# A perceiver layer on one core: a state scan written over its input, half of its products on GpSimd, and a small matmul moved to the end of its step

## The chip, the cores and the metric

The kernel runs on one core of a Trainium2 chip. The core has five engines with an instruction stream each: PE (TensorE, matrix products; PEld is its loading of weights), DVE (VectorE), ACT (ScalarE), POOL (GpSimd) and SP (SyncE, which here only issues DMAs). Each engine runs its own instructions in order; semaphores make one wait for another. The metric is the device time in microseconds (us) of one execution.

## The reference: what is computed

Three blocks follow each other on x, 16 sequences of 128 rows by 512 columns, all in float32:

- cross attention: queries from x (normalised), keys and values from a context of 2048 rows for each sequence, 16 heads of 32 columns;
- a Mamba block and an MLP: a projection in to 1024 channels, a causal convolution, the selective state scan, a projection out, a normalisation, a GELU MLP of 2048, and a normalisation;
- a feed-forward block with a shared product and a gated expert product.

The change is in the state scan. In the reference it is

```python
deltaA = jnp.exp(dt[..., None] * A)
deltaBx = dt[..., None] * Bm[:, :, None, :] * x[..., None]
def step(h, xs):
    dA, dBx, C = xs
    h = dA * h + dBx
    y = jnp.einsum('bdn,bn->bd', h, C)
    return (h, y)
```

with 16 states (n) for each of the 1024 channels (d). The scan runs over the 128 rows of a sequence. Every scan step below is one DVE instruction over many rows, not one row.

## The kernel before, in words

**The loop.** All work is laid out by hand in one loop over u (lines 1329 to 1460). Attention takes the first 256 steps (NU = 256): step u handles four heads of 512 context rows. The Mamba block runs behind it. Its 8 groups (g) of two sequences each have 32 scan steps (r), and group g's step r stands in step u = 32 (g + 1) + 22 + r. So scan steps begin at u = 54, run beside attention, and go on through u = 309. From u = 257 on there is no attention; the MLP and feed-forward products ("feeds", line 1355) are given out over the steps instead, and this part, to the end, is called the tail.

**The engines' order.** Each engine runs what the loop issues for it in the loop's order. What happens at which step beside the fixed parts is written in tables (`late`, `behind`, `after`, `inner` and others, lines 1203 to 1269), filled by `put(where, u, function)`.

**One attention step on PE** (in this order): the four scores (L307) into banks[0] to banks[3], at the same time in four row groups of the array; the weighted values of the step before (L385, `avp`); two key or value products into `pa` and `pc` (L244, `x_products`); the transposes of three heads' probabilities back into banks[0] to banks[2] (L357); late products, such as in-projections (L577) or out-projections (L515, L762); and the last one or two key or value products (`y_products`). The fourth head's probabilities go another way: DVE transposes blocks (L337, `tr`), SP stores them to HBM (L341, `trd`) and SP gathers them one step later (L347, `pd`).

**One attention step on DVE**: four maxima over the score banks (L315), the first half scan, sums that read `pc` (L264 for keys, L274 for values), the block transpose, the second half scan, the sums after `y_products`, and what the tables add. On ACT: exponentials (L325), decays (L719), copies of the transposed probabilities (L359), and copies of `pa`.

**One scan step** (lines 692 to 755) covers four states of 128 channels for two sequences, in two halves i = 0, 1 of two states (128 x 512 elements). GpSimd makes w = dt x B (L698) one step ahead, ACT writes the decays into PSUM (L719), DVE scans (L733), DVE multiplies by C (L736), and GpSimd sums over the states (L745, L749). B and C come as broadcasts from HBM (`bc`, L647). The decays lie in the bank `hst`; in the tail the second half has `pc`. Decays are written from column 1 on; column 0 of each sequence must be zero, and `anew` (L712) sets it by a memset of four columns. Since the scan is written over the decays, this is done after every half scan:

```python
flat = h.rearrange("p n t -> p (n t)")
nc.vector.tensor_tensor_scan(
    flat, flat, w.rearrange("p n t -> p (n t)"), 0.0, ALU.mult, ALU.add
)
nc.vector.tensor_tensor(
    w, h, bcs[g * 32 + r, DS][:, i * NH // 2 : (i + 1) * NH // 2, :], ALU.mult
)
anew(h)
```

There are 512 half scans. `anew` is also called once for `hst` before the loop (L1325) and once for `pc` at u = 256 (L1268).

**The time step's product** (`dt_first`, L662 to L675; put into `behind` at L1244) is made once in four scan steps, at u = 3 mod 4: one matmul of 128 x 256 (L665, two PE rows in the profile) into a PSUM bank, then two ACT instructions (L669, L670), one on DVE (L672, the reader of the bank beside L669) and one on GpSimd (L674). `dt_second` (L679, L681) and `dt_third` (L686 to L689) follow in the next two steps. In the loop, `behind` stands after the late products and ahead of `after`, `inner` and the step's `y_products`. During attention its bank is `banks[3]` where no late product has taken it, else `pc`.

The functions that the diff touches and what calls them:

Of the kernel before, what the change touches and what calls it, by code (L numbers as in the profile page):

```python
# [10 lines left out]
ALU = mybir.AluOpType  # L11
# [9 lines left out]
DI, DS, DTR = 1024, 16, 32  # L21
# [9 lines left out]
NH = 4  # L31
# [5 lines left out]
def perceiver_layer(ctx: ExitStack, tc: tile.TileContext, a: dict, out: bass.AP):  # L37
    nc = tc.nc
# [74 lines left out]
    with ExitStack() as es:  # L113
# [15 lines left out]
        banks = [psum.tile([P, 512], FP, tag=f"s{j}", name=f"bank{j}") for j in range(4)]  # L129
# [3 lines left out]
        pc = psum.tile([P, 2, 256], FP, tag="pc", name="pc")  # L133
# [148 lines left out]
        def hold(key, g, pa, tag):  # L282
            n = ND if tag == "tr" else 1
            t = pool.tile([P, 2 * n, 256], FP, tag=tag, name=f"{tag}{key}{g}", bufs=1)[:, 0:2, :]
            nc.scalar.copy(t, pa)
            held[key] = t
# [4 lines left out]
        def y_products(of, g, ph, pa, pc):  # L291
            for i, ps in (((6, pa),), ((3, pc), (4, pa)))[ph]:
                product(of, g, i, ps)

        def y_sums(of, g, ph, pa, pc, tag="u2"):
            if ph == 0:
                hold(of + "u2", g, pa, tag)
            else:
                sums[of](g, 0, 1, pc, held[of + "u2"])
                sums[of](g, 1, 0, None, pa)  # L300
# [237 lines left out]
        zTs, xas, zss, bcs, dts, wts, ysum, wts_in = ({} for _ in range(8))  # L538
# [79 lines left out]
        def silu_second():  # L618
            for v, t in sgs:
                nc.vector.scalar_tensor_tensor(t, v, 0.0, t, ALU.min, ALU.subtract)  # L620
# [85 lines left out]
        def states(g, r, i):  # L706

            return pc if i and 32 * (g + 1) + LAG + r > NU else hst

        def anew(h):  # L710

            nc.vector.memset(h.rearrange("p n (b t) -> p (n b) t", b=GB)[:, :, 0:1], 0.0)  # L712
# [16 lines left out]
        def scan(g, r, i):  # L729
            ec, q = divmod(r, 4)  # L730
            w, h = wts[g, r][i], states(g, r, i)
            flat = h.rearrange("p n t -> p (n t)")
            nc.vector.tensor_tensor_scan(  # L733
                flat, flat, w.rearrange("p n t -> p (n t)"), 0.0, ALU.mult, ALU.add
            )
            nc.vector.tensor_tensor(  # L736
                w, h, bcs[g * 32 + r, DS][:, i * NH // 2 : (i + 1) * NH // 2, :], ALU.mult
            )
            anew(h)

            if q == 0 and i == 0:
                ysum[g, ec] = w
            elif (q, i) == (0, 1):
                s = ssm.tile([P, 2, GT], FP, tag="ysum", name="ysum", bufs=1)
                nc.gpsimd.tensor_tensor(s, ysum[g, ec], w, ALU.add)  # L745
                ysum[g, ec] = s
            else:
                s = ysum[g, ec]
                nc.gpsimd.tensor_tensor(s, s, w, ALU.add)  # L749
            if (q, i) == (3, 1):  # L750
                y = ysum[g, ec][:, 0, :]
                nc.gpsimd.tensor_tensor(y, y, ysum[g, ec][:, 1, :], ALU.add)
                nc.gpsimd.tensor_tensor(y, y, xas[g, ec], ALU.add)
                nc.gpsimd.tensor_tensor(zss[g, ec], y, zss[g, ec], ALU.mult)
                del ysum[g, ec], xas[g, ec], dts[g, ec]
# [44 lines left out]
        def flat(ps):  # L800
            return ps.rearrange("p k q -> p (k q)")
# [3 lines left out]
        def bank():  # L805
            return free_banks.pop(0)

        def give_back(*ps):
            free_banks.extend(ps)
# [393 lines left out]
        late, after, inner, middle, loads, head, behind, between, weights = ({} for _ in range(9))  # L1203
# [27 lines left out]
        for g in range(NG):  # L1231
            p = 32 * (g + 1)
# [87 lines left out]
        ps = banks[2]  # L1320
# [8 lines left out]
        for u in range(last):  # L1329
            live = u < NU  # L1330
            g, r = divmod(u - 32 - LAG, 32)
# [3 lines left out]
            makes = 0 < made < B * SB  # L1335
# [64 lines left out]
            if scans:  # L1400
                scan(g, r, 0)
# [16 lines left out]
            free = banks[NP:]  # L1418
# [14 lines left out]
            if scans:  # L1433
                scan(g, r, 1)
            for f in middle.get(u, ()):
                f()
            for f, ps in zip(after_turns, places):
                if live:
                    f(ps)
                else:  # L1440
                    ps = bank()
                    f(ps)
                    give_back(ps)
            for f in behind.get(u, ()):
                n = len(late.get(u, ()))
                if live and n < len(free):
                    ps = free[n]
                else:
                    ps = flat(pc) if makes else banks[2] if live else bank()
                f(ps)  # L1450
                if not live:
                    give_back(ps)
            for f in after.get(u, ()):
                f()
            for f in inner.get(u, ()):
# [1 line left out]
            if makes:  # L1457
                y_products(of, made, phase, pa, pc)
                y_sums(of, made, phase, pa, pc)
            silu_second()  # L1460

        while fed < len(units):
# [74 lines left out]
```

## Time and profile before

| what | before |
|---|---|
| median of three timed runs | 3677.24 us (3677.19 to 3677.81) |
| the profiled execution's own time | 3673.68 us |
| its span, first to last instruction | 3671.8 us |
| PE, DVE, ACT, POOL busy | 3622.8, 2704.5, 2422.8, 2135.5 us |
| granted PE clock, mean | 0.997 |
| HBM | 185 GB/s over the span |

How to read it: a row of the costliest groups names the line, engine and operation, what is written and read, the count, then the busy time of the group in us and the mean length of one in ns, and at the end the idle time of the engine just ahead of these instructions with what ended most of it. A row of a timeline has the start in us, the length in us, engine, line and operation, and in brackets the idle time ahead and what ended it. Matmuls overlap, so PE's busy time is a union, and a mean length of a matmul is longer than its share of the time.

### The profile page before, as it was taken

Reading aid. Unit: us, or ns where it says so; the run is one execution under the profiler, and the core shown is the slowest. Engines: PE = TensorE matmul, PEld = TensorE weight load, DVE = VectorE, ACT = ScalarE, POOL = GpSimd, SP = SyncE. Lnnn points to the kernel's source line nnn. Section 1 sums busy time; section 2 is a strip of 40 time slices with the busy share of each in tenths; the row PEclk is TensorE's granted clock in tenths of the full one; section 3 lists DMA queues with packets and bytes.
Section 4 is the critical chain, followed back from the end, with each engine's and each line's share of the span. In section 5 each row is a group of like instructions: output and inputs, shape, how many; then the busy total and the mean of one; then the engine's idle time right before and its main releaser. Section 6 shows DMA issues by size and latency. Waiting matters only on the chain. (4 is left out here: it accounts for less than half of the span.)

```text
span 3671.8 us, 70944 instructions
## 1 busy us (share of the span) xinstructions
PE 3622.8 (99%) x25096; PEld 2750.8 (75%) x25096; DVE 2704.5 (74%) x4902; ACT 2422.8 (66%) x5928; POOL 2135.5 (58%) x2097
## 2 busy tenths in 40 slices
PE   9999999999999999999999999999999989999999
PEld 7878787778777877788778877887778766655655
DVE  4444445897879787878788878887887768778843
ACT  4555556787777776777687767776777675545422
POOL 2111214675767676766676667766776657667720
PEclk9999999999999999999999999999999999999999
DMA  3322333665666666665666575657565678576752
GB/s 122 99 90 94 106 108 127 193 200 185 203 199 193 194 188 212 196 197 171 223 196 193 171 243 171 220 162 229 186 213 171 216 233 312 193 278 232 269 176 75
DMA packets 527554, 682.74 MB, mean 186 GB/s; under 512 B 44848, under 2 KB 378960, under 8 KB 526944
## 3 DMA queue, kind: packets, MB, share of 16 engines
q1 hardware_dynamic: 526752, 677.57, 57.0%
q8 instruction: 200, 3.28, 0.3%
q14 instruction: 154, 1.26, 0.1%
q0 software_dynamic: 448, 0.63, 0.1%
HBM read 594.40 MB, written 83.62 MB: 185 GB/s over the span
## 5 line engine op out<-in xcount | busy, mean ns | idle before, releaser
L315 DVE TENSOR_REDUCE nm<-bank 128x1 f32<-128x512 f32 x1024 | 635.4, 682 | 229.2 <-PE bank L307 228.9
L749 POOL TENSOR_TENSOR ysum<-ysum,w 128x512 f32<-128x512 f32 x384 | 501.1, 1305 | 422.9 <-DVE hst L712 258.7
L325 ACT ACTIVATE pr<-bank,nm 128x512 f32<-128x512 f32 x1024 | 689.1, 686 | 66.9 <-DVE nm L315 62.0
L698 POOL TENSOR_TENSOR w<-dx,bc 128x512 f32<-128x512 f32 x512 | 653.2, 1297 | 29.3 <-DMA bc<-bcd 20.9
L733 DVE TENSOR_TENSOR_SCAN hst<-hst,w 128x512 f32<-128x512 f32 x459 | 556.7, 1213 | 38.5 <-ACT hst L719 34.2
L719 ACT ACTIVATE hst<-dt,alog 128x254 f32<-128x254 f32 x918 | 440.1, 479 | 88.9 <-DVE hst L712 70.7
L359 ACT COPY pT<-bank 128x512 f32<-128x512 f32 x768 | 396.5, 587 | 43.6 <-PE bank L357 43.4
L357 PE MATMUL bank<-ident,pr 128*128 128x128 f32 x3072 | 378.2, 273 | 0.8 <-ACT pr L325 0.7
L357 PEld LDWEIGHTS bank<-ident,pr 128*128 128x128 f32 x3072 | 350.5, 141 | 26.3 <-ACT pr L325 3.0
L385 PEld LDWEIGHTS avp<-pT,v 128*32 128x32 f32 x6144 | 207.0, 110 | 196.1 <-issue 193.4
L736 DVE TENSOR_TENSOR w<-hst,bc 128x512 f32<-128x512 f32 x459 | 317.5, 692 | 22.2 <-DMA bc<-bcd 6.5
L307 PE MATMUL bank<-kt,qT 32*128 32x512 f32 x2048 | 305.0, 641 | 5.2 <-ACT pT L359 5.2
L236 POOL TENSOR_TENSOR t<-c,c 128x512 f32<-128x512 f32 x128 | 163.2, 1275 | 239.2 <-PE pc L244 235.1
L385 PE MATMUL avp<-pT,v 128*32 128x128 f32 x6144 | 276.7, 276 | 0.8 <-ACT pT L359 0.7
L244 PE MATMUL pa<-t,ks 128*128 128x256 f32 x1024 | 248.6, 386 | 0.0
L244 PE MATMUL pa<-vs,t 128*128 128x256 f32 x1008 | 244.7, 386 | 0.0
L244 PEld LDWEIGHTS pa<-t,ks 128*128 128x128 f32 x1024 | 185.9, 190 | 36.0 <-issue 11.5
L244 PEld LDWEIGHTS pa<-vs,t 128*128 128x128 f32 x1008 | 185.5, 190 | 34.8 <-issue 10.1
L325 ACT ACTIVATION_READ_ACCUMULATOR pr<-bank,nm 128x1 f32 x1024 | 208.5, 204 | 0.0
L385 PE MATMUL avp<-pd,v 128*32 128x128 f32 x1536 | 204.5, 276 | 0.0
L577 PE MATMUL bank<-zT,win 128*128 128x256 f32 x808 | 185.1, 379 | 0.0
L236 POOL TENSOR_TENSOR t<-c,t 128x512 f32<-128x512 f32 x128 | 163.7, 1279 | 31.7 <-issue 11.9
(321 smaller groups left out, 7392.2 us busy)
## 6 DMA issues: line engine op xcount, KB each, us to landing
bc<-bcd SPq DMA_DIRECT2D x512, 512.0 KB, 4.9
c<-in_ctxT_dram SPq DMA_DIRECT2D x256, 256.0 KB, 5.9
trd<-tr SPq DMA_DIRECT2D x256, 256.0 KB, 4.4
pd<-trd SPq DMA_DIRECT2D x1024, 64.0 KB, 1.9
wf<-in_w_dram SPq DMA_DIRECT2D x124, 512.0 KB, 7.0
wqo<-in_wqkvo_dram SPq DMA_DIRECT2D x128, 256.0 KB, 5.4
win<-in_win_dram SPq DMA_DIRECT2D x128, 256.0 KB, 5.0
wout<-in_wout_dram SPq DMA_DIRECT2D x128, 256.0 KB, 5.9
```

Of the source, the lines that this page charges most:

```text
L236: nc.gpsimd.tensor_tensor(t, x, y, ALU.subtract)
L244: nc.tensor.matmul(ps[:, r, :], l[:, kc, r * P : (r + 1) * P], m[:, kc, :], start=(i in (1, 2, 5) and r == 0 and kc == 0), stop=(r == 1 an ...
L315: nc.vector.tensor_reduce(stats[b][0][j][:, sb, hg : hg + 1], banks[j], AX.X, ALU.max, negate=True)
L325: nc.scalar.activation(pr[:, j, :], banks[j], AF.Exp, bias=nm[j][:, sb, hg : hg + 1], accum_out=sm[:, sb, h : h + 1],)
L357: nc.tensor.transpose(ps[:, i, :], prs[u][:, j, i * P : (i + 1) * P], ident)
L359: nc.scalar.copy(pT, ps)
L385: nc.tensor.matmul(avp[j * HD : (j + 1) * HD, v % 4, :], values(v, i, j), pts[v, j][:, i, :] if j < NP else pds[v][:, :, j - NP, i, :], st ...
L698: nc.gpsimd.tensor_tensor(w, dx.unsqueeze(1).to_broadcast([P, NH // 2, GT]), bcs[g * 32 + r, 0][:, i * NH // 2 : (i + 1) * NH // 2, :], AL ...
L719: nc.scalar.activation(bt(h[:, k, :])[:, :, 1:], bt(dt)[:, :, 1:], AF.Exp, scale=aneg[:, ec, n : n + 1],)
L733: nc.vector.tensor_tensor_scan(flat, flat, w.rearrange("p n t -> p (n t)"), 0.0, ALU.mult, ALU.add)
L736: nc.vector.tensor_tensor(w, h, bcs[g * 32 + r, DS][:, i * NH // 2 : (i + 1) * NH // 2, :], ALU.mult)
L749: nc.gpsimd.tensor_tensor(s, s, w, ALU.add)
```

## The change

Two edits.

- In `scan`, the result goes over w (SBUF) instead of over the decays (PSUM). The product with C then reads w and the broadcast C, both in SBUF, and is made on GpSimd for the first half and on DVE for the second. The memset after each half scan is gone; the zeros of `hst` and `pc` are set once and stay.
- In the loop, the functions in `behind` (the time step's product) are called after `y_products` and `y_sums` instead of ahead of `after`. During attention their bank is `pc` while key and value products are made, and banks[2] in the last attention steps; banks[3] is no longer used for it.

```diff
         def scan(g, r, i):
             ec, q = divmod(r, 4)
             w, h = wts[g, r][i], states(g, r, i)
-            flat = h.rearrange("p n t -> p (n t)")
+            x = w.rearrange("p n t -> p (n t)")
             nc.vector.tensor_tensor_scan(
-                flat, flat, w.rearrange("p n t -> p (n t)"), 0.0, ALU.mult, ALU.add
+                x, h.rearrange("p n t -> p (n t)"), x, 0.0, ALU.mult, ALU.add
             )
-            nc.vector.tensor_tensor(
-                w, h, bcs[g * 32 + r, DS][:, i * NH // 2 : (i + 1) * NH // 2, :], ALU.mult
+            (nc.vector if i else nc.gpsimd).tensor_tensor(
+                w, w, bcs[g * 32 + r, DS][:, i * NH // 2 : (i + 1) * NH // 2, :], ALU.mult
             )
-            anew(h)
...
-            for f in behind.get(u, ()):
-                n = len(late.get(u, ()))
-                if live and n < len(free):
-                    ps = free[n]
-                else:
-                    ps = flat(pc) if makes else banks[2] if live else bank()
-                f(ps)
-                if not live:
-                    give_back(ps)
             for f in after.get(u, ()):
                 f()
             for f in inner.get(u, ()):
                 f()
             if makes:
                 y_products(of, made, phase, pa, pc)
                 y_sums(of, made, phase, pa, pc)
+            for f in behind.get(u, ()):
+                ps = flat(pc) if makes else banks[2] if live else bank()
+                f(ps)
+                if not live:
+                    give_back(ps)
             silu_second()
```

## The prediction, made before the changed kernel was run

> **What bounds the kernel now.** I read the page first: the profiled execution took 3673.68 us around a span of 3671.8 us, 3.56 us below the median of the three timed runs (3677.24 us). All sums below are changes against that one execution; I apply them to the median.
>
> ```profile
> PE 3622.8 (99%) x25096; PEld 2750.8 (75%) x25096; DVE 2704.5 (74%) x4902; ACT 2422.8 (66%) x5928; POOL 2135.5 (58%) x2097
> L749 POOL TENSOR_TENSOR ysum<-ysum,w 128x512 f32<-128x512 f32 x384 | 501.1, 1305 | 422.9 <-DVE hst L712 258.7
> L698 POOL TENSOR_TENSOR w<-dx,bc 128x512 f32<-128x512 f32 x512 | 653.2, 1297 | 29.3 <-DMA bc<-bcd 20.9
> L733 DVE TENSOR_TENSOR_SCAN hst<-hst,w 128x512 f32<-128x512 f32 x459 | 556.7, 1213 | 38.5 <-ACT hst L719 34.2
> L736 DVE TENSOR_TENSOR w<-hst,bc 128x512 f32<-128x512 f32 x459 | 317.5, 692 | 22.2 <-DMA bc<-bcd 6.5
> ```
>
> The reader is to see two things. PE is busy for all but 49 us of the span, so whatever the other engines save, the time can only fall by the places where PE waits. And GpSimd (POOL) waits 258.7 us for the memset L712, the last of the three DVE instructions (scan, product, memset) of each half scan.
>
> So I went through the timeline of PE for the places where a group starts late. From the first scan step to the last attention step (about 615 to 2960 us) there are few kinds. The first, PE and then DVE, around one step's scores:
>
> ```profile
> 2185.26 1.14 PE L307 MATMUL bank<-kt,qT 32*128 32x512 f32 x8
> ...
> 2194.46 1.56 PE L307 MATMUL bank<-kt,qT 32*128 32x512 f32 x8
> ```
> ```profile
> 2194.38 0.48 DVE L672 TENSOR_SCALAR dt<-bank,dtb 128x256 f32<-128x256 f32 x1
> ```
>
> The eight rows of the scores take 1.14 us, but 1.56 us in the step after a time-step product that went to banks[3]: the fourth score must wait until L672 has read that bank, at 2194.86 us. I count 20 such steps, each 1.56 instead of 1.14 us: three of every 32 steps, those where no late product held the free bank.
>
> The second kind, once in 32 steps (six times), is the product into pc two steps after a sequence's end:
>
> ```profile
> 1886.75 1.99 PE L244 MATMUL pc<-c,ks 128*128 128x256 f32 x8 [0.94 <-DVE kt L264]
> ```
> ```profile
> 1883.77 1.22 DVE L733 TENSOR_TENSOR_SCAN hst<-hst,w 128x512 f32<-128x512 f32 x1
> 1885.02 0.69 DVE L736 TENSOR_TENSOR w<-hst,bc 128x512 f32<-128x512 f32 x1
> 1885.79 0.06 DVE L712 MEMSET hst<- 128x4 f32 x1
> 1885.82 0.88 DVE L264 SCALAR_TENSOR_TENSOR kt<-pc,bk,u1k 128x256 f32<-128x256 f32 x2
> ```
>
> PE starts about 1.1 us late, because L264, which empties pc, stands behind scan, product and memset. The third is one wait of 4.71 us at step 253, where DVE's product waits 4.57 us for the broadcast C. By the table of windows, of PE's 49 us of idle time 8.3 lie in the first 50 us, 9 between 640 and 2960, 11.6 between 2960 and 3020 (the 4.71 among them) and 20 in the tail after that. (The late fourth score is no idle time: the other three rows of the array run.)
>
> **The change, part by part.** *Time-step product behind the step's last product.* It is one matmul (two PE rows) before and after; the order of the program shows it moved behind the product into pa, and always into pc while key and value products are made. The fourth score no longer shares a bank with it: 20 x 0.42 = **-8.4 us**. What is late next: pc is written again 3.9 us into the next step, and L672 and ACT's L669 have read it by about 1.3 us, so nothing. ACT's two instructions (0.49 and 0.42 us) move behind the copy of pa, into the next step's start, where ACT idles 0.64 us before avs; the exponentials slip about 0.25 us, and the transposes that need them come 2.5 us later. If that cover failed it would cost 0.25 us x 50 steps = 12 us. GpSimd's u (L674) and DVE's L679 slip with them, unneeded until the step after. It issues no DMA. At step 255 it goes to banks[2] instead of banks[3] and must wait for a copy: at most its own 0.43 us.
>
> *The scan writes over w.* Its row is 1213 ns into PSUM; no row has it into SBUF. From the rows that differ only so, 692 ns for L736 with a PSUM operand and 692 ns for L1022 alone with none, I take 0, with +-20 ns x 512 = 10 us of DVE time as ends, nearly all beside PE. The 512 memsets go: 62 ns and about 80 ns of waiting each. ACT's next decays are then free at the scan's end, 0.83 us sooner.
>
> *First half's product to GpSimd.* DVE loses 256 x 0.692 = 177 us. GpSimd gains 256 products of two SBUF inputs; the nearest rows are L698 and L749, 1.30 us: 333 us. Per 32 steps (1859.01 to 2237.97 us) POOL is busy 260.3 of 379.0 us; 32 x (1.30 + 0.08 wait for its own result) makes it 304. Much of it fits in the wait for DVE that L749 shows: product, then sum, while DVE scans the second half (1.21 us). Behind it on GpSimd stand the context sums for PE. The narrowest is step 165, where t2 ends at 5.65 us and PE wants it at 6.95 us; there the chain starts from DVE's second product, which does not move, so I charge 0. If it did, each 1 us past the margin costs two steps in 32, 12 us in all.
>
> The second half's product stays on DVE, but now reads two SBUF tensors. The trace has such a pair:
>
> ```profile
> 3175.38 0.69 DVE L1022 TENSOR_TENSOR xr<-xr,x 128x512 f32<-128x512 f32 x1
> ```
> ```profile
> 3269.65 1.64 DVE L1022 TENSOR_TENSOR xr<-xr,x 128x512 f32<-128x512 f32 x1
> ```
>
> The first ran while GpSimd was idle, the second while it multiplied (and GpSimd's two L698 took 2.94 instead of 2.50 us). L736 with its PSUM input never left 691 to 694 ns. So each of the 256 remaining products waits 0 to 0.95 us, and GpSimd loses up to 0.69 us per step. On DVE that gives back 0 to 243 us of the 177 + 73 us saved. It comes at the step's end, where DVE idles 0.3 to 1.5 us before the next maxima.
>
> The Trainium skill's GPSIMD Engine Reference, section Engine selection, speaks against the change: elementwise work belongs on VectorE, being about twice as slow on GpSimd. The rows agree on the price, 1305 against 692 ns; by the rule alone 256 x 0.61 = 157 us would be lost. SBUF — State Buffer, section Who interferes with whom, calls the shared read port a lock for a whole instruction; by that the worst wait would be GpSimd's full 1.30 us, 333 us over 256.
>
> *What this leaves of the other waits.* At the six pc waits the chain is 0.83 us shorter: up to -5.0 us. But just ahead stand two small DVE instructions with two SBUF inputs (L483, 0.99 us, and L490, 0.61 us), which already wait for GpSimd, now busier: up to +1.3 us each time, +8. I take **-1 us**. At step 253 the product that waits is now GpSimd's, so ACT and PE go on: up to -4.7 us, and PE's slow stretch after it, at most -3 us. But the next weighted product needs pd:
>
> ```profile
> 2973.81 1.74 SPq L347 DMA_DIRECT2D pd<-trd  x4
> ```
>
> This is issued when the previous transfer lands, whatever DVE does; with the page's 1.9 us to landing it is there at 2977.4 us, and PE came to it at 2978.33 us. So **-1 us**. SP's next broadcast of C must wait for GpSimd's product as well, up to about 6 us into a step; the transfer behind it, trd, is not ready before 7.3 us: 0.
>
> *Tail (57 steps).* The long wait at 3201.3 us is for the copy of xd behind DVE's two halves: 0.8 us sooner, and up to 3 us more if PE's slow stretch after it goes; **-1 us**. Against it stands POOL. From 3260 to 3400 us it is busy 111.7 of 140 us with 16.5 steps; 16.5 x (1.38 + 0.69) makes 146. About 6 us too many, part of which DVE's lighter load and its 20 us of idle time cover: **+2 us**, between 0 and the 20 us of the rival below.
>
> Sum: -8.4 - 1 - 1 - 1 + 2 = -9.4, rounded to **-10 us**: 3663.7 for the profiled execution, **3667 us** for the median.
>
> **Rivals.** (1) *The port takes it back.* The wait of DVE's product lands on the six pc waits and on ACT's path in short steps; 8 us of losses meet 8.4 of gain: about 3676 us, within 3670 to 3684. For it: 102 of 128 L620 began with GpSimd running. Against it: DVE gains 0.83 us ahead of every place where PE waits on it. (2) *Slower: GpSimd becomes the bound in the tail.* If GpSimd cannot hold the pace from 3020 to 3100 and 3260 to 3400 us (79.5 of 80 and 146 of 140 us by the sum above), DVE's scan waits for w, and the FFN work queued behind it on DVE keeps PE's banks; 25 steps x 0.9 us = 22, less 10: 3689 us. It decides once POOL's work per step passes the 8.5 us that a step lasts there. Against it: PE has seven banks of slack, and POOL idles 28 us in that window. (3) *More goes than I count:* all six pc waits, step 253's wait with its slow stretch, and the slow stretch at 3204: -8.4 - 5 - 6 - 4 = -23: 3654 us.
>
> **How the numbers follow.** Forecast (3660 to 3670 us) 0.46; rival 3, 0.14; rival 1, 0.25; rival 2, 0.15. A measurement of this kernel tells 0.2% from no change, 7.4 us. Faster is forecast and rival 3, 0.60; the same is rival 1, 0.25; slower rival 2, 0.15. The range runs from just under rival 3 to rival 1's middle, 3652 to 3679 us, leaving out rival 2 and a fifth of rival 1.
>
> **What would show it.** Right: scores at 1.14 us after every step, L665 into pc alone, second-half L736 between 0.69 and 1.64 us, POOL near 2500 us, PE's idle time in 615 to 2960 us smaller. Wrong: PE waiting for t (L236) or pT in the short steps, DVE's L733 waiting for POOL's w, new PE waits after 3020 us.

## The result, and the profile after

The changed kernel is a little slower, not faster: 3685.70 us median (12 runs, 3679.97 to 3688.74) against 3677.22 us for the kernel before (12 runs, 3674.89 to 3680.99). The ratio is 1.0021, with a 95% interval of 1.0012 to 1.0030: about 8 us, just over the 0.2% that can be told from no change. The profiled execution of the changed kernel took 3679.97 us (span 3678.2 us), the fastest of its 12, 6.29 us above the profiled execution of before.

Behind `scan` the changed kernel's lines are one lower: L748 is the sum that was L749, L954 the feed-forward product that was L955, L819 the load that was L820. The same rows of the page, after (busy time of each engine; then groups with count, busy us, mean ns, idle time ahead and its main releaser):

```profile
PE 3624.0 (99%) x25096; PEld 2746.4 (75%) x25096; DVE 2572.5 (70%) x4134; ACT 2415.9 (66%) x5928; POOL 2501.2 (68%) x2353
...
L748 POOL TENSOR_TENSOR ysum<-ysum,w 128x512 f32<-128x512 f32 x384 | 503.7, 1312 | 149.3 <-DVE w L736 118.4
L733 DVE TENSOR_TENSOR_SCAN w<-hst,w 128x512 f32<-128x512 f32 x459 | 552.1, 1203 | 51.1 <-ACT hst L719 48.4
...
L736 POOL TENSOR_TENSOR w<-w,bc 128x512 f32<-128x512 f32 x256 | 341.1, 1332 | 65.4 <-DVE w L733 65.3
...
L736 DVE TENSOR_TENSOR w<-w,bc 128x512 f32<-128x512 f32 x256 | 236.4, 923 | 9.6 <-DMA bc<-bcd 0.8
```

The engines' totals are as forecast: GpSimd at 2501.2 us, the scan into SBUF no slower (1203 against 1213 ns), GpSimd's wait for the memset gone. The row to stop at is the last one. A product that always took 692 ns with its PSUM input takes 923 ns on average with two SBUF inputs; 125 of the 256 take over 0.75 us, the longest 1.81 us. DVE has 132 us less to do, and PE is as busy as before.

Where the time went is read from the distances of PE's instructions between the two traces. I cut the run into four stretches: up to the scores of step 64; from there to step 250; the end of attention, to the first feed-forward product (L954); and the tail, to the last sixteen expert products. In the profiled executions they changed by -0.3, -1.5, +1.7 and +7.6 us, and what is behind by -1.2.

**Attention stage.** The late fourth score is gone. PE, the scores after such a step:

```profile
2183.40 1.14 PE L307 MATMUL bank<-kt,qT 32*128 32x512 f32 x8
...
2192.08 0.59 PE L665 MATMUL pc<-xd,dtw 128*128 128x256 f32 x2
2192.60 1.14 PE L307 MATMUL bank<-kt,qT 32*128 32x512 f32 x8
```

1.56 us is 1.14 again, and L665 goes into pc. Steps 0 and 28 of each 32 are shorter by 0.42 us. Step 8 gains only 0.23 us on average: ahead of its maxima (at step 136) DVE's product takes 1.31 us in place of 0.69, and L561, the normalisation of x, 1.05 in place of 0.55. And step 18 of each 32 is longer, in all six places. The starts of the scores of such a step and of the next one, before and then after:

```profile
2073.47 1.14 PE L307 MATMUL bank<-kt,qT 32*128 32x512 f32 x8
...
2087.43 1.14 PE L307 MATMUL bank<-kt,qT 32*128 32x512 f32 x8
```
```profile
2070.39 1.14 PE L307 MATMUL bank<-kt,qT 32*128 32x512 f32 x8
...
2085.52 1.14 PE L307 MATMUL bank<-kt,qT 32*128 32x512 f32 x8
```

13.96 us has become 15.13. DVE's timeline at this place, before and after, shows why:

```profile
2073.45 0.69 DVE L736 TENSOR_TENSOR w<-hst,bc 128x512 f32<-128x512 f32 x1
2074.19 0.22 DVE L483 TENSOR_TENSOR sm<-sm,nm 128x64 f32<-128x64 f32 x1
...
2076.44 2.47 DVE L315 TENSOR_REDUCE nm<-bank 128x1 f32<-128x512 f32 x4
```
```profile
2070.36 1.14 DVE L736 TENSOR_TENSOR w<-w,bc 128x512 f32<-128x512 f32 x1
2071.43 1.30 DVE L483 TENSOR_TENSOR sm<-sm,nm 128x64 f32<-128x64 f32 x1
...
2074.86 2.47 DVE L315 TENSOR_REDUCE nm<-bank 128x1 f32<-128x512 f32 x4
```

L483 is tiny and has two SBUF inputs. Before, it started while GpSimd was idle between two sums and took 0.22 us; after, it starts beside the first of GpSimd's two sums and takes 1.30. The maxima (L315) start 4.47 us into the step and not 2.97, the exponentials wait for them, and PE's transposes wait for the exponentials. GpSimd's timeline, before and after:

```profile
2072.58 1.28 POOL L749 TENSOR_TENSOR ysum<-ysum,w 128x512 f32<-128x512 f32 x1
2074.29 1.28 POOL L749 TENSOR_TENSOR ysum<-ysum,w 128x512 f32<-128x512 f32 x1 [0.43 <-DVE hst L712]
```

```profile
2069.68 1.28 POOL L736 TENSOR_TENSOR w<-w,bc 128x512 f32<-128x512 f32 x1
2071.03 2.96 POOL L748 TENSOR_TENSOR ysum<-ysum,w 128x512 f32<-128x512 f32 x2
```

The added product stands where the first sum stood, and both sums now fall into the next step.

**Tail.** From 3400 to 3500 us PE was busy without a break before (100.00 us of 100); after, it has two long waits there, at 3426 and 3497 us, both for feed-forward weights (each from its own view of PE's timeline):

```profile
3426.27 6.59 PE L954 MATMUL pa<-mT,wf 128*128 128x256 f32 x16 [3.25 <-DMA wf<-in_w_dram]
3432.69 3.62 PE L954 MATMUL bank<-mT,wf 128*128 128x256 f32 x16
```
```profile
3497.80 7.15 PE L954 MATMUL bank<-mT,wf 128*128 128x256 f32 x32 [1.77 <-DMA wf<-in_w_dram]
```

The first costs twice: 3.25 us of waiting, and then 16 products that take 6.59 us where the next 16 take 3.62. The profile shows the granted PE clock at 0.50 during these 16 (3426.3 to 3432.1 us), and at 1.00 in the same window before. Measured on the starts of the feed-forward products, the kernel falls back by 6.7 us at the first wait and by 2.0 at the second; all else in the tail comes to -1.1 us. Both loads went out late. SP's issues of a broadcast and of the weights behind it, before and then after; these are the weights of the first wait:

```profile
3409.90 1.04 SPq L647 DMA_DIRECT2D bc<-bcd  x2
3410.99 1.22 SPq L820 DMA_DIRECT2D wf<-in_w_dram  x2
```
```profile
3416.89 2.24 SPq L647 DMA_DIRECT2D bc<-bcd  x2
3419.18 1.22 SPq L819 DMA_DIRECT2D wf<-in_w_dram  x2
```

The weights stand behind a broadcast in SP's order; they are issued 8.2 us later than before, and those of the second wait 12.8 us later (3490.51 and not 3477.68 us). What the broadcast waits for, by the view of SP's waits (us in total, times, longest), before from 3390 to 3425 us and after from 3395 to 3430 us:

```profile
SPq L647 <- POOL w L698: 16.7, 5, 6.1
```

```profile
SPq L647 <- POOL w L698: 21.6, 4, 6.4
```

GpSimd has not yet read the tile that the broadcast is to overwrite. The wait is not new: it grew. In the window of the second line, 3395 to 3430 us, the kernel before has 10.6 us of it, the longest 4.3. From 3400 to 3500 us GpSimd was busy 74.87 us before; it is busy 95.29 us after, all but full.

### The profile page after: what moved, and what is told of

Same layout as the page of the kernel before. It is cut to its first block, busy times and chain, and to the rows that moved or that the text cites. A ratio compares the mean times of both kernels' runs of the same rounds, so it can differ in the third digit from the quotient of the medians.

```text
span 3678.2 us, 70467 instructions
## 1 busy us (share of the span) xinstructions
PE 3624.0 (99%) x25096; PEld 2746.4 (75%) x25096; DVE 2572.5 (70%) x4134; ACT 2415.9 (66%) x5928; POOL 2501.2 (68%) x2353
## 4 chain that ended last, share of the span: by engine, by line
PE 87%; DVE 4%; ACT 3%; POOL 3%; DMA 2%; issue 1%; SPq 0%; DVEq 0%; POOLq 0%
PE pa L244 23%; PE pc L244 17%; PE bank L357 8%; PE bank L307 7%; PE avp L385 7%; PE bank L577 5%; PE bank L985 3%; PE bank L761 2%; PE bank L954 2%; PE bank L1086 2%; PE bank L515 2%; ACT pr L325 1%; POOL w L698 1%; PE pa L954 1%; PE bank L442 1%
## 5 line engine op out<-in xcount | busy, mean ns | idle before, releaser
L315 DVE TENSOR_REDUCE nm<-bank 128x1 f32<-128x512 f32 x1024 | 635.6, 683 | 205.0 <-PE bank L307 204.7
L698 POOL TENSOR_TENSOR w<-dx,bc 128x512 f32<-128x512 f32 x512 | 652.9, 1296 | 32.7 <-DMA bc<-bcd 24.3
L748 POOL TENSOR_TENSOR ysum<-ysum,w 128x512 f32<-128x512 f32 x384 | 503.7, 1312 | 149.3 <-DVE w L736 118.4
L733 DVE TENSOR_TENSOR_SCAN w<-hst,w 128x512 f32<-128x512 f32 x459 | 552.1, 1203 | 51.1 <-ACT hst L719 48.4
L736 POOL TENSOR_TENSOR w<-w,bc 128x512 f32<-128x512 f32 x256 | 341.1, 1332 | 65.4 <-DVE w L733 65.3
L307 PE MATMUL bank<-kt,qT 32*128 32x512 f32 x2048 | 296.0, 640 | 0.5 <-ACT pT L359 0.5
L736 DVE TENSOR_TENSOR w<-w,bc 128x512 f32<-128x512 f32 x256 | 236.4, 923 | 9.6 <-DMA bc<-bcd 0.8
L264 DVE SCALAR_TENSOR_TENSOR kt<-pc,bk,u1k 128x256 f32<-128x256 f32 x256 | 112.2, 480 | 173.5 <-PE pc L244 104.6
L274 DVE TENSOR_TENSOR v<-pc,u1v 128x512 f32<-128x512 f32 x126 | 87.2, 692 | 177.2 <-ACT u1v L285 90.9
```

Of the source, the lines that this page charges most:

```text
L307: nc.tensor.matmul(banks[j], qts[b][rows, hg, :], kts[u // 4, hg][rows, :], start=True, stop=True)
L315: nc.vector.tensor_reduce(stats[b][0][j][:, sb, hg : hg + 1], banks[j], AX.X, ALU.max, negate=True)
L698: nc.gpsimd.tensor_tensor(w, dx.unsqueeze(1).to_broadcast([P, NH // 2, GT]), bcs[g * 32 + r, 0][:, i * NH // 2 : (i + 1) * NH // 2, :], AL ...
L733: nc.vector.tensor_tensor_scan(x, h.rearrange("p n t -> p (n t)"), x, 0.0, ALU.mult, ALU.add)
L736: (nc.vector if i else nc.gpsimd).tensor_tensor(w, w, bcs[g * 32 + r, DS][:, i * NH // 2 : (i + 1) * NH // 2, :], ALU.mult)
```

## The experiments

Each kernel was run beside the kernel before on the same chip. The times together; the last three columns are the change of a stretch against before, in us, from the one profiled execution of each. The attention column (steps 64 to 250) leaves step 22 of each 32 out: PE mostly waits there for a weight transfer (`wqo`), and the six of them together moved by -1.9 to +3.1 us without following the edit.

| kernel | median us | before, median us | ratio, 95% interval | attention | end of attention | tail |
|---|---|---|---|---|---|---|
| changed | 3685.70 | 3677.22 | 1.0021 (1.0012 to 1.0030) | +0.4 | +1.7 | +7.6 |
| 1 move only | 3667.32 | 3674.64 | 0.9983 (0.9974 to 0.9992) | -6.5 | +2.0 | +0.4 |
| 2 scan only | 3691.07 | 3674.64 | 1.0045 (1.0032 to 1.0059) | +7.5 | +2.3 | +8.7 |
| 3 tail products on DVE | 3680.05 | 3674.64 | 1.0014 (1.0005 to 1.0022) | -0.8 | +1.9 | +5.8 |
| 4 broadcasts behind weights | 3680.75 | 3674.64 | 1.0016 (1.0008 to 1.0025) | -0.8 | +2.4 | +6.2 |
| 5 both products on DVE | 3679.74 | 3673.68 | 1.0016 (1.0007 to 1.0025) | -2.5 | +2.3 | +3.9 |
| 6 second half in PSUM | 3671.45 | 3673.68 | 0.9992 (0.9983 to 1.0001) | -5.8 | +0.9 | +4.3 |
| 7 move, last one in place | 3667.53 | 3673.68 | 0.9983 (0.9974 to 0.9992) | -6.5 | -0.5 | -0.6 |
| 8 steps 1 and 17 as before | 3670.69 | 3673.68 | 0.9994 (0.9985 to 1.0002) | -10.6 | +1.0 | +6.4 |
| 9 changed scan in step 2 only | 3664.70 | 3674.61 | 0.9973 (0.9962 to 0.9983) | -9.1 | +1.1 | +0.2 |
| 10 tail as before | 3673.38 | 3674.61 | 0.9998 (0.9990 to 1.0007) | -0.1 | +4.5 | -0.3 |
| 11 steps 1, 17 and tail as before | 3662.48 | 3674.61 | 0.9967 (0.9956 to 0.9978) | -9.6 | +2.1 | -0.6 |
| 12 the same, last one in place | 3663.63 | 3675.13 | 0.9968 (0.9957 to 0.9978) | -10.6 | +2.9 | -1.7 |

**1. The move alone.** `scan` as before, `behind` as changed.

> The scan as in the kernel before (in PSUM, both products on VectorE, memsets); only the time step's product moved behind the step's last product. Theory (the move is worth its 20 late fourth scores and nothing else happens; the loss comes from the scan part, most of it in the tail): 8.4 us faster than before, 3668 to 3670 us, all 50 score groups at 1.14 us, steps 18 of each 32 unchanged at 13.95 us, no PE wait for wf in the tail. Rival (the move itself costs, through the later transposes at step 18 and the move to banks[2] at step 255): at step 18 15.1 us as in the changed kernel, and 3676 us or more.

The theory holds: about 7 us faster, step 18 at 13.95 us, nothing lost in the tail.

**2. The scan alone.** `scan` as changed, `behind` as before.

> Only the scan part (written over w, no memset, first half's product on GpSimd); the time step's product where it was. Theory (the two parts add up: the whole is 8.5 us slower, the move 8.4 us faster): 17 us slower than before, 3692 to 3696 us, step 18 of each 32 at 15.1 us, PE waits for wf in the tail. Rival (the two parts overlap: with the scan part the fourth score is not what ends the step): 3684 to 3688 us.

16.4 us slower, as the theory said. The two parts add up: 0.9983 and 1.0045 make 1.0028, within the interval of the whole. So the change is one good edit and one bad one, and the bad one loses about equally in attention and in the tail.

**3. Tail: both products on DVE, over w.**

```diff
-            (nc.vector if i else nc.gpsimd).tensor_tensor(
+            (nc.vector if i or 32 * (g + 1) + LAG + r > NU else nc.gpsimd).tensor_tensor(
```

> The changed kernel, but after the last attention step both products are on VectorE; GpSimd has 57 of them fewer. Theory (GpSimd is the bound in the tail and its lateness costs PE about 8 us between 3400 and 3500 us): the waits for wf are gone, 3675 to 3678 us, about 8 to 10 us less than the changed kernel. Rival (the tail's loss comes from the state it is entered in, after the transition, or from the scan over w itself): within 3 us of the changed kernel, 3683 to 3688 us.

Between the two (the tail has 53 scan steps, so GpSimd has 53 products fewer, not 57): the long waits for wf are gone, but only 2 to 3 us come back. In their place PE's transposes of a row (L925) wait for DVE's normalisation of it (L851). PE's waits from 3400 to 3500 us, the largest:

```profile
PE bank L925 <- DVE xr L851: 2.0, 2, 1.1
```

And DVE's products, which stand ahead of L851 on DVE, have become longer:

```profile
L736 DVE TENSOR_TENSOR w<-w,bc 128x512 f32<-128x512 f32 x309 | 291.4, 943 | 10.7
```

Taking GpSimd's product away is not enough. The products that DVE gets read two SBUF tensors and take 943 ns on average where one with a PSUM input took 692; just ahead of L851 two of them take 1.19 and 1.71 us, and a scan waits 1.16 us for GpSimd's w.

**4. Tail: a step's broadcasts issued behind the weights that it feeds.**

```diff
-            if not 1 <= u <= NU:
+            if u < 1:
                 step_loads()
...
                     feed(fed)
                     fed += 1
+                step_loads()
                 if scans:
                     decays(g, r, 0)
```

> The changed kernel, but in the tail a step's broadcasts of B and C are issued on SP behind the weight loads that this step feeds, and not ahead of them; GpSimd's work is the same. Theory (GpSimd's lateness reaches PE through SP's queue: the broadcast waits until GpSimd has read its tile, and wf stands behind it): the PE waits of 3.41 and 1.93 us for wf go or shrink below 1 us, 3677 to 3681 us. Rival (GpSimd's lateness reaches PE by several ways; take one and the next holds it): the waits for wf go but PE waits for scans, rows or banks instead, 3683 to 3688 us.

The rival's mechanism. The time, 3680.75 us, lies just inside the theory's range; but its own kernel before was 2.6 us faster than the one that the ranges were made from, which puts it at the lower end of the rival's. No wait for wf is left between 3400 and 3500 us, so SP's order did carry GpSimd's lateness to PE. But the tail still loses 6.2 us, with the next holder as in 3:

```profile
PE bank L925 <- DVE xr L851: 2.7, 2, 2.2
```

Here DVE's scan had waited 4.80 us at 3458.08 us for GpSimd's w (L698), with L851 queued behind it: the very path that rival 2 of the prediction named.

**5. Both products on DVE over w, everywhere.**

```diff
-            (nc.vector if i else nc.gpsimd).tensor_tensor(
+            nc.vector.tensor_tensor(
```

> The changed kernel with both halves' products on VectorE, over w; GpSimd's list is that of the kernel before. Theory (in the attention stage the price is GpSimd's 199 added products, whose sums slip into the way of DVE's small two-SBUF instructions; in the tail it is the shared port, which both DVE products now need): the attention stage gains the 8 us of the move as in the move alone, step 18 of each 32 is back at 13.95 to 14.3 us, the tail loses about 5 us: 3 us faster than before to level with it. Rival (the port is the price in the attention stage as well): step 18 stays above 14.5 us and the time is 3 us or more above before.

A miss in the total: 6 us above before, as the rival said, with step 18 nearly back (14.2 us), as the theory said. GpSimd's list is what it was (the changed kernel adds 203 products to it ahead of the tail, not 199), but the products pay for the second SBUF input, 183 of the 512 with more than 0.75 us:

```profile
L736 DVE TENSOR_TENSOR w<-w,bc 128x512 f32<-128x512 f32 x512 | 475.0, 928 | 24.9 <-DMA bc<-bcd 7.3
```

928 against 692 ns is 121 us of DVE time, and step 2 of each 32 is longer by 0.4 us. So GpSimd's added work is not the whole price.

**6. Second half in PSUM as before, first half's product on GpSimd.**

```diff
-            x = w.rearrange("p n t -> p (n t)")
+            x = h if i else w
...
+            if i:
+                anew(h)
```

> The changed kernel, but the second half is scanned in PSUM and multiplied from there, with its memset, as before; only the first half is scanned over w and multiplied on GpSimd. Theory (GpSimd's added work is the price): DVE's product is back at 0.69 us, but step 18 of each 32 stays at 14.8 us or more, PE still waits for wf in the tail, and the time is 5 to 8 us above before. Rival (the port wait of DVE's own product is the price): step 18 at 13.95 us and the time 3 us below before to level with it.

By the total the rival is right: 2 us below before by the medians, which the interval does not tell from level, and 10 below the changed kernel, with GpSimd's 256 products in place. DVE's product again:

```profile
L741 DVE TENSOR_TENSOR w<-hst,bc 128x512 f32<-128x512 f32 x203 | 140.4, 692 | 7.0
```

The 53 in the tail take 691 ns. By the place the theory keeps a part: step 18 is 14.6 us, 0.7 above before, because L483 still meets GpSimd's sums (1.09 to 1.20 us). So of the 1.17 us lost in that step 0.7 are left without the second product's wait, and 0.2 without GpSimd's added work (5); the two do not add up to the whole. The tail still loses 4.3 us with GpSimd's added work and DVE's product in PSUM, and 3.9 with both products on DVE over w (5).

**7. The move, with step 255's product left in the free bank.**

```diff
-                ps = flat(pc) if makes else banks[2] if live else bank()
+                ps = flat(pc) if makes else free[0] if live else bank()
```

> The move alone, with the last of its products, at step 255, left in the free bank as before and not in banks[2]. Theory (that one product's wait for the copy of its bank, 2.4 us, is a loss on PE's path): 2 us less than the move alone, 8 to 9 us faster than before. Rival (what PE does next waits for transfers anyway): the same as the move alone, 6 to 7 us faster than before.

The rival: the same ratio as the move alone. In the trace L665's wait of 2.37 us is gone; where it went is shown in 12.

**8. Steps 1 and 17 of each 32 as before.** In 16 of the 256 scan steps the scan, both products and the memset are those of before.

```diff
+            old = (32 * (g + 1) + LAG + r) % 16 == 1
+            x = h if old else w
```

> The changed kernel, but in steps 1 and 17 of each 32 the scan is as before (in PSUM, both products on VectorE, memsets): 16 of the 256 scan steps. Theory (GpSimd's product in these steps pushes its two sums into the next step, where DVE's small two-SBUF instructions L483 and L490 lie ahead of the maxima): step 18 back at 13.95 us, 7 us less than the changed kernel, about level with before. Rival (GpSimd is behind by the sum of its work, not by this step's): step 18 above 14.5 us and less than 3 us gained.

Step 18 is back at 13.95 us, and L483 at 0.22 us. The kernel is 2 to 3 us below before by the medians, which the interval does not quite tell from level, though the tail still loses 6.4 us. Against the changed kernel it gains more than the 7 us of the theory, since step 2 gains too, 0.6 us each time: there L264 no longer stands behind product and memset, and L483 ahead of the maxima takes 0.85 us; the changed kernel, with 1.30 there, gains 0.1. PE's scores at step 18 (this kernel is some 9 us ahead of before here):

```profile
2064.24 1.14 PE L307 MATMUL bank<-kt,qT 32*128 32x512 f32 x8
...
2078.19 1.14 PE L307 MATMUL bank<-kt,qT 32*128 32x512 f32 x8
```

**9, 10, 11. What is worth keeping.**

```diff
+            old = 32 * (g + 1) + LAG + r > NU or (32 * (g + 1) + LAG + r) % 32 != 2    # 9
+            old = 32 * (g + 1) + LAG + r > NU                                          # 10
+            old = 32 * (g + 1) + LAG + r > NU or (32 * (g + 1) + LAG + r) % 16 == 1    # 11
```

Kernel 9 has the edit of 7 as well.

> The move, its last product left in the free bank at step 255, and the changed scan in steps 2 of each 32 alone (the steps where PE waits for kt behind the first half's scan); every other scan, the tail's too, as before. Theory (the terms add: 6.5 us for the move, 3.4 us for step 2 as in the run with steps 1 and 17 as before, 2 us at step 255): 10 to 13 us faster than before. Rival (step 2 gains only because GpSimd is early in all of the steps around it, and step 255 gains nothing): as the move alone, 6 to 7 us faster.

> The changed kernel up to the last attention step; behind it the scan as before (in PSUM, both products on VectorE, memsets). Theory (the tail's 7 us come from the scan over w there, by the port and by GpSimd's added products, each of which alone leaves 4 to 6 us of it): level with before to 2 us above it, 6 to 8 us less than the changed kernel. Rival (the tail loses because of the phase in which it is entered): 4 us or more above before.

> The changed kernel with the scan as before in steps 1 and 17 of each 32 and in the tail. Theory (the two places are all that the changed scan loses): 9 to 11 us faster than before. Rival (more places lose, or what was gained in the attention stage is waited for at its end): as steps 1 and 17 alone, about 3 us faster.

All three came out on the theory's side, each at most 1.2 us outside the bounds given against before (9.9 us faster for 9, 1.2 for 10, 12.1 for 11, by the medians). In 9 the total is partly luck: of its three terms, step 2 gave 2.2 us in the profile and not 3.4, and step 255 gave nothing (7, 12). With the tail as before the tail's loss is gone (10); with steps 1 and 17 as before as well, the kernel is 12 us faster than before (11). Those two places hold nearly all that the changed scan loses; step 8 still gains 0.27 us and not 0.42. Kernel 11 beats both kernels of the case.

**12. Kernel 11 with step 255's product left in place.**

> The kernel with the scan as before in steps 1 and 17 of each 32 and in the tail, and the last moved product, at step 255, left in the free bank and not in banks[2]. Theory (its 2.4 us wait is on PE's path): 2 us less than the same kernel with banks[2], 13 to 15 us faster than before. Rival (transfers behind it take its place, as the equal medians of the move with and without it suggest): 11 to 13 us faster than before, the same as with banks[2].

The rival again, 11.5 us. PE in kernel 11, then in kernel 12:

```profile
2985.38 1.22 PE L665 MATMUL bank<-xd,dtw 128*128 128x256 f32 x2 [2.37 <-ACT pT L359]
...
2999.14 7.10 PE L962 MATMUL bank<-mT,wf 128*128 128x256 f32 x18 [4.51 <-DMA wf<-in_w_dram]
```
```profile
2996.14 1.26 PE L385 MATMUL avp<-pd,vh 128*32 128x128 f32 x8 [2.99 <-DMA pd<-trd]
...
3001.51 8.80 PE L962 MATMUL bank<-mT,wf 128*128 128x256 f32 x27 [4.11 <-DMA wf<-in_w_dram]
```

With the bank's wait gone PE waits for pd, and in both kernels over 4 us for wf behind it. The wait at 255 is covered by transfers: removing it leaves the ratio as it is (1 and 7, 11 and 12).

## Why the prediction was wrong, point by point

- **The move, -8.4 us: right.** With the move alone, steps 0, 8 and 28 became shorter by 0.38 to 0.42 us each, and the kernel 7 us faster. Its product at step 255 waited 2.37 us instead of the "at most 0.43" I gave it: the bank was waited for from ACT's copy of the last transposes. By runs 7 and 12 this costs nothing that can be measured.
- **The scan into SBUF, 0: right** (1203 ns).
- **The port's wait "comes at the step's end, where DVE idles 0.3 to 1.5 us before the next maxima": this is the step that failed in the attention stage.** The size was bounded about rightly (0.69 to 1.64 us; measured up to 1.81, mean 0.92). The place was not looked through. I had seen L483 and L490 wait for GpSimd in step 2 of each 32 and took that for their only place. They stand in step 18 too, where before L483 took 0.22 us, started while GpSimd was idle. DVE has no idle time there between the second product and the maxima to take up a delay, so the longer product (1.14 us in place of 0.69) and the longer L483 (1.30) went on to PE: 6 x 1.17 = 7.0 us, as much as the move gave. L490 did not change (0.74 to 0.75 us there in every run). Run 8 took the loss away by changing 16 steps. Step 8, with L561, is a smaller place of the same kind; there the scan alone (2) costs 0.48 us each time. In the attention stage this is rival 1 in size, a loss that meets the move's gain (+0.4 us in all), but in other places than it named.
- **The six pc waits, -1 us: right in the sum** (-0.6 us in the profile; -3.4 in run 8, where L483 takes 0.85 us in place of 1.30), with other parts than I gave: L483 grew by 0.3 us and not 1.3, and of the 0.83 us that the chain became shorter L264 lost 0.4 again by waiting for ACT (L285, 0.41 us at step 130).
- **Step 253, -1 us: about right in its reason, wrong in size.** Scores came earlier, and PE waited 4.33 us for pd in place of 4.71 for the scores. From step 253 to 255 the changed kernel took 1 us more, not less. The end of attention varied by 5 us between the kernels' profiled executions, and by 3 us among the changed kernel, 3, 4 and 10, which run the same program up to there (+1.7 to +4.5); I would now call it 0 with that spread.
- **The tail, "+2 us": mis-sized; it measured +7.6. This is the second step that failed.** The sum that I made (146 us of GpSimd work in 140, from 3260 to 3400 us) did not come true there: GpSimd was busy 131.79 us, and PE idled less than before. GpSimd was all but full later, from 3400 to 3500 us. What failed is the place and the price, and the sentence that SP's broadcast waiting for GpSimd costs "0". I argued that from trd, which is an attention transfer. In the tail the transfers behind the broadcast are the weights, and those PE waits for. Nor had I a term for a new stretch at half the PE clock behind a wait, which makes up nearly half of the 6.7 us lost at 3426 us. The other term, -1 us at 3201 us, was right in kind: PE's wait there fell from 2.86 to 1.45 us, the stretch at half clock behind it (0.50 from 3203 to 3209.7 us) is at 1.00, and the kernel gained 1.6 us, after it had lost 1.9 in short waits ahead of it. Rival 2 had the right cause and sign, but named only the way through DVE's scan; the first to be late was SP's queue, and DVE's scan came second (4). Its price, 22 us before the gain, was three times too high.
- *The sum by stretches* of the profiled execution: -0.3 to step 64, +0.4 in attention with -1.9 in step 22, +1.7 at its end, +7.6 in the tail, -1.2 behind: +6.3 us, which is what the two profiled executions differ by. The medians differ by 8.5; the further 2 us lie within the spread of the changed kernel's executions (3679.97 to 3688.74), of which the profiled one is the fastest, and I have no trace of a longer one.

The Trainium skill's SBUF — State Buffer, section Who interferes with whom, says that a DVE instruction with two SBUF inputs contends with a GpSimd instruction that reads SBUF, and that one with at most one SBUF input, outside the modes that use both of DVE's ports, does not. The products agree on both sides: 928 ns mean in run 5, 691 and 692 ns in run 6 beside GpSimd's full list. L561 has one SBUF tensor as input and still went from 0.55 to 1.05 us in step 8; no run shows whether it ran in such a mode. The prediction had the rows for the products (L1022 and L736); it failed by not asking the same of every small instruction on DVE's path.

What stays open: which part of the tail's loss is GpSimd's work and which the port. Each alone leaves about 4 us (runs 6 and 5), both together 7.6, and each was seen with another wait at PE, so a sum of single waits is not to be had. A part of it is the clock: between 3400 and 3500 us the granted PE clock falls to 0.50 for 6.8 us in the changed kernel and for 3.4 us in runs 3, 4, 6 and 8, each time around a wait of PE, and not at all in the others. It is not needed for the loss: run 2 has none there and loses 8.7 us in the tail. No experiment separates it from the waits.

## What to carry to other kernels

When work moves to GpSimd, list every DVE instruction with two SBUF inputs, the tiny ones first, and look for those that are short only because GpSimd is idle just then; here an operand left in PSUM was worth more than the memset that it costs (run 6, 10 us below the changed kernel). When an engine gets near its limit in a stage, ask which DMA queue waits for it and what stands behind in that queue: it need not be the same transfer in every stage. And try the parts of a change one by one and place by place: here 12 of the steps before the tail and the 53 steps of the tail hid a version 12 us faster than before inside one 8 us slower.

## What the runs showed of the hardware that I had not expected

- The wait does not go by the size of the instruction that waits: L483, 128 x 64 elements, took 0.22 us when it started while GpSimd was idle, and 1.29 to 1.30 us in all twelve places of the attention stage behind GpSimd's 1.3 us instructions. Its group's mean went from 510 to 1095 ns.
- It hits GpSimd as well: its product took 1332 ns on average, 1287 in run 6, where DVE's product has a PSUM input.
- A wait of PE of 3.25 us was followed by 16 products in 6.59 instead of 3.62 us, 3 us more, at a granted clock of 0.50; the wait of 1.77 us at 3497 us was followed by products at their normal pace (32 in 7.15 us). The length of the wait alone does not decide it: in run 2 PE waited 3.02 us at 3437 us and the next 16 products took 3.69 us at a clock of 1.00, while in run 4 a wait of 2.07 us at 3190 us was followed by 3.4 us at 0.50.
